# A transformer layer on one core: the beginning written out by hand, the next batch's latents transposed later, and the last weight loads moved

## The chip, the cores and the metric

The kernel runs on one NeuronCore of a Trainium2 chip. The metric is the device time of one execution in microseconds (us); the median of several runs counts, and lower is better.

## The reference

The layer works on 8 batches of 512 tokens with 512 features, in float32: a layer norm, a multi-head attention with low-rank latents, a residual, a second layer norm, a gated feed-forward network (FFN), and a second residual. Cut to what matters:

```python
b, s, _ = hidden_states.shape                    # 8, 512; hidden_states is the normed x
q    = rmsnorm(hidden_states @ wq_a.T, q_norm_w)      # 384 latents for the queries
q    = (q @ wq_b.T).reshape(b, s, 16, 192)            # 16 heads: 128 plain, 64 rotary
kv   = hidden_states @ wkv_a.T                        # 128 latents and 64 rotary
kv_c = rmsnorm(kv[..., :128], kv_norm_w)
k_pe = rope(kv[..., 128:])                            # one rotary key, shared by the heads
kv_x = (kv_c @ wkv_b.T).reshape(b, s, 16, 256)        # per head: 128 key, 128 value
attn = softmax(concat(q_nope, rope(q_pe)) @ concat(k_nope, k_pe).T * SCALE)
x    = x + (attn @ v).reshape(b, s, 2048) @ wo.T
# second half: x + down(silu(gate(norm(x))) * up(norm(x))), weights rounded to fp8 e4m3
```

## The kernel before

**Weights are folded.** The up-projections of keys and queries are multiplied together once per head (`fold_q`, tile `wa`), so that a head's queries are formed directly from the 384 latents and scored against the 128 key latents. In the same way the value up-projection and the output projection are multiplied (`fold_o`, tile `wst`). A group `g` is four heads; its `wst` is stored to DRAM in batch 0 and loaded again by every later batch (`load_wst`, four pieces, two buffers).

**The attention is one long list of steps.** A step is one tile of 128 queries of one head of one batch: `at(b, h, t)` is its number, 8 x 16 x 4 = 512 steps. Each step issues a score tile (`scores`: three matmuls on TensorE into a PSUM tile `sc`, a row maximum on VectorE, an exponential on ScalarE), and, at the start of the next step, `rest`: reciprocal, scaling, and a block-wise transpose on VectorE into `block`. After every second step `send` writes `block` to a DRAM scratch (`way<-block`) and reads it back in four pieces (`prT<-way`), which finishes the transposition of the probabilities. All of these transfers are issued by SP, in order, and each `prT` issue waits until its `way` has landed. Six steps after a head's last tile `attend` multiplies the values with `prT` (`av`).

**Other work is attached to steps by hand.** `put(i, f)` appends a piece of work to step `i`, and under a manual schedule the engines get their instructions in exactly that order. Once per batch the *next* batch's latents are formed this way: `center`, `transpose_x` and `project_x` (tile `lr_ps`) at heads 7, 8, 11 and 12; `norms` at head 13; `scale(t)` on VectorE at (13, 2) for the first two token tiles and two steps later for the other two; and one step after `scale` its `transpose_l(t)`: four TensorE transposes into a PSUM tile `lat_pt`, which ScalarE copies into `lat`. All single-bank PSUM tiles (`sc`, `av`, `qn_ps`, `qpe_ps`, `lr_ps`, `lat_pt` and others) share one pool of six buffers. The output products of a group (`z_ps`, `u_ps`, `v_ps`) have two further buffers.

**The beginning** (latents of batch 0, first folds, first rotary part) stands ahead of the manual schedule, so the framework's scheduler orders it. Its loads all go through SP: the first token tile of `x`, the four chunks of the latent weights `wlr`, then the other three tiles of `x`, then the rest. There is one standard deviation for all four tiles, and `xT` has one buffer.

**The end.** While the last batch's last heads run, SP also loads the last group's `wst` pieces and the first FFN weights (`load_ffn`: four tiles `wg`, one behind each group, then `wu`). Two gate tiles of the FFN (`pg<-yh,wg`) are issued on TensorE ahead of the last head's `attend`.

The lines that place this work are:

```python
put(at(b - 1, 13, 2) + t // 2 * 2, p["scale"], t)            # VectorE
put(at(b - 1, 13, 3) + t // 2 * 2, p["transpose_l"], t)      # TensorE, ScalarE
put(at(b, G * g + 3, 3) - 6 + 2 * k, f)                      # piece k of wst
put(at(B - 1, G * g + 3, 1), self.load_ffn, "wg", g, wp, f"wa{g}")
```

Of the kernel before, what the change touches and what calls it, by code (L numbers as in the profile page):

```python
# [43 lines left out]
P = 128  # L44
# [42 lines left out]
class Layer:  # L87
# [45 lines left out]
    def ln_stats(self, x, small):  # L133


        nc = self.nc
        st = small.tile([P, NT, 6], F32, tag="ln_st", name="ln_st")
        mv = small.tile([P, NT, 2], F32, tag="ln_mv", name="ln_mv")
        sd = small.tile([P, NT], F32, tag="ln_sd", name="ln_sd")
        rstd = small.tile([P, NT], F32, tag="ln_rstd", name="ln_rstd")  # L140

        def moments(t):
            nc.vector.bn_stats(st[:, t, :], x[:, t, :])
            nc.vector.bn_aggr(mv[:, t, :], st[:, t, :])

        def deviation():
            nc.scalar.activation(sd, mv[:, :, 1], AF.Sqrt, bias=self.eps_ln)

        def deviation_inverse():
            nc.vector.reciprocal(rstd, sd)  # L150

        return moments, deviation, deviation_inverse, mv, rstd

# [116 lines left out]
    def attention(self):  # L270
        tc, nc, ins, wp, xp = self.tc, self.nc, self.ins, self.wp, self.xp
        with ExitStack() as ctx:
# [21 lines left out]

            x = xp.tile([P, NT, H], F32, tag="x", name="x")
            wlr = self.wlr
            nc.sync.dma_start(x[:, 0, :], hidden(0)[:, 0, :])
            for c in range(NC):
                nc.sync.dma_start(wlr[:, c, :], ins["wlr"][:, c, :])
            for t in range(1, NT):  # L300
                nc.sync.dma_start(x[:, t, :], hidden(0)[:, t, :])
            xs, toks = {0: x}, {0: wp.tile([P, NT, RQ + 2 * DR], F32, tag="tok", name="tok")}
            qnw, knw, knr = self.load_w("qnw"), self.load_w("knw"), self.load_w("knr")
            self.gs, self.us = self.load_w("gs"), self.load_w("us")
# [114 lines left out]
            def latents(b):  # L419


                lat = xp.tile([P, NR + 1, S], F32, tag="lat", name=f"lat_{b}", bufs=2)
                kvt = hp.tile([P, NT, RKV], F32, tag="kvt", name=f"kvt_{b}")
                kpe = hp.tile([P, 2, S], F32R, tag="kpe", name=f"kpe_{b}")


                tok = toks.pop(b)
                x = tok if b else xs[0]
                ss = sp.tile([P, 2, NT], F32, tag="ss", name="ss", bufs=1)
                rms = sp.tile([P, 2, NT], F32, tag="rms", name="rms", bufs=1)  # L430
                got = {}
                moments, deviation, deviation_inverse, mv, rstd = self.ln_stats(x, sp)

                def center(t):
                    got[t] = hp.tile([P, H], F32, tag="xn", name="xc", bufs=1)
                    nc.vector.tensor_scalar(got[t], x[:, t, :], mv[:, t, 0:1], None, ALU.subtract)

                def transpose_x(t):
                    pt = self.ln_transposed(got.pop(t), ps_r)
                    got["xT"] = hp.tile([P, NC, P], F32, tag="xT", name="xT", bufs=1)  # L440
                    nc.scalar.copy(got["xT"], pt)

                def project_x(t):
                    xT = got["xT"]
                    for k, (lo, hi, n) in enumerate(((0, RQ, RQ), (RQ, RL, RKV))):
                        ps = ps_r.tile([P, hi - lo], F32, tag="r", name="lr_ps")
                        for c in range(NC):
                            nc.tensor.matmul(  # L448
                                ps, xT[:, c, :], wlr[:, c, lo:hi], start=c == 0, stop=c == NC - 1
                            )  # L450

                        r = rstd[:, t : t + 1]
                        if k == 0:
                            nc.vector.tensor_scalar(tok[:, t, :RQ], ps, r, None, ALU.mult)
                        else:
                            nc.vector.tensor_scalar(kvt[:, t, :], ps[:, :RKV], r, None, ALU.mult)
                            for d in (RQ, RQ + DR):
                                nc.vector.tensor_scalar(tok[:, t, d : d + DR], ps[:, RKV:], r, None, ALU.mult)
                        nc.scalar.activation(
                            ps[:, :n], ps[:, :n], AF.Square, scale=r, accum_out=ss[:, k, t : t + 1]  # L460
                        )

                def norms():
                    for k, n in enumerate((RQ, RKV)):
                        nc.scalar.activation(
                            rms[:, k, :], ss[:, k, :], AF.Sqrt, bias=self.eps_rms, scale=1.0 / n
                        )

                def norms_inverse():
                    nc.vector.reciprocal(rms, rms)  # L470

                def scale(t):
                    nc.vector.tensor_scalar(
                        tok[:, t, :RQ], tok[:, t, :RQ], rms[:, 0, t : t + 1], None, ALU.mult
                    )
                    nc.vector.tensor_scalar(
                        kvt[:, t, :], kvt[:, t, :], rms[:, 1, t : t + 1], None, ALU.mult
                    )

                def transpose_l(t):  # L480
                    pt = ps_r.tile([P, NR + 1, P], F32, tag="r", name="lat_pt")
                    for r in range(NR):
                        nc.tensor.transpose(pt[:, r, :], tok[:, t, r * P : (r + 1) * P], self.ident)
                    nc.tensor.transpose(pt[:, NR, :], kvt[:, t, :], self.ident)
                    nc.scalar.copy(lat[:, :, t * P : (t + 1) * P], pt)

                def rotary():
                    pt = ps_r.tile([P, NT, P], F32, tag="r", name="kpe_pt")
                    for t in range(NT):
                        nc.tensor.transpose(pt[:, t, :], tok[:, t, RQ:], self.ident)  # L490
                    r = rope(pt.rearrange("p t s -> p (t s)"), SCALE)
                    nc.scalar.copy(kpe[:, 0, :], r)
                    nc.gpsimd.tensor_tensor(kpe[:, 1, :], r, kpe[:, 0, :], ALU.subtract)

                pieces = {
                    f.__name__: f
                    for f in (
                        moments, deviation, deviation_inverse, center, transpose_x, project_x,
                        norms, norms_inverse, scale, transpose_l, rotary,
                    )  # L500
                }
                return pieces, (lat, kvt, kpe)
# [152 lines left out]
            def put_q(b, h):  # L655

                i = at(b, h)
                if h % 2 == 0:
# [3 lines left out]
                            put(i - 5 + k, f)  # L662

                    put(i - 6, rotary_part)
                put(i - 4, project, b, h)


            p0, state["latents", 0] = latents(0)
            p0["moments"](0), p0["center"](0)
            for t in range(1, NT):  # L670
                p0["moments"](t)
            p0["deviation"](), p0["deviation_inverse"]()
            for t in range(NT):
                p0["transpose_x"](t)
                if t + 1 < NT:
                    p0["center"](t + 1)
                p0["project_x"](t)
            p0["norms"](), p0["norms_inverse"](), p0["scale"](0)
            for t in range(NT):
                p0["transpose_l"](t)  # L680
                if t + 1 < NT:
                    p0["scale"](t + 1)
            load_q(0)
            times = load_pe(0)
            cs_s = self.load_w("cs")
            fold_q(0)
            times()
            load_q(1)
            p0["rotary"]()
            for f in project_pe(0, 0):  # L690
                f()
            project(0, 0)
            fold_q(1)
            load_q(2), load_q(3), load_o(0)


            for b, h in ((b, h) for b in range(B) for h in range(NH)):
# [35 lines left out]
            for b in range(1, B):  # L733
                for g in range(NG):
                    for k, f in enumerate(load_wst(b, g)):
                        put(at(b, G * g + 3, 3) - 6 + 2 * k, f)
                for k, f in enumerate(load_x(xs, b, hidden(b), xp, "x")):
                    put(at(b, 5) + k, f)

# [15 lines left out]
            def put_latents(b):  # L755
# [7 lines left out]
                put(at(b - 1, 13, 1), p["norms_inverse"])  # L763
                for t in range(NT):
                    put(at(b - 1, 13, 2) + t // 2 * 2, p["scale"], t)
                    put(at(b - 1, 13, 3) + t // 2 * 2, p["transpose_l"], t)
                put(at(b - 1, 14, 2), p["rotary"])

            def put_ffn():
# [10 lines left out]
                    put(at(b - 1, 0, 1) + 2 * k, f)  # L780
                put(at(b - 1, 3), *((put_latents, b) if b < B else (put_ffn,)))
            for g in range(NG):
                put(at(B - 1, G * g + 3, 1), self.load_ffn, "wg", g, wp, f"wa{g}")
            put(at(B - 1, NH - 1, 3) + 4, self.load_ffn, "wu", 0, wp, "wst", 2)

            self.gates = {}
# [3 lines left out]
            )  # L790

            with tc.manual_schedule():
                prT = block = rest = None
                for i in range(len(steps) + 19):
                    if rest:
# [144 lines left out]
```

## Time and profile before

| what | us |
|---|---|
| median of 3 runs | 2797.75 |
| the 3 runs | 2793.24, 2797.82, 2797.75 |
| the profiled execution, its own time | 2792.89 |
| its span, first to last instruction | 2791.1 |
| TensorE (PE) busy | 2725.8 (98%) |
| VectorE (DVE) busy | 1883.9 (67%) |
| ScalarE (ACT) busy | 898.1 (32%) |
| GpSimd (POOL) busy | 597.8 (21%) |

The span is 1.8 us shorter than the execution's own time. The attention fills the span up to about 2270 us, the FFN the rest. A float32 matmul is two records of the trace, so "x6" behind a matmul group means three matmuls. PE's busy time is an upper bound, because ends of pipelined matmuls are modelled; the list of waits shows where PE stood still.

### The profile page before, as it was taken

Reading aid. Unit: us, or ns where it says so; the run is one execution under the profiler, and the core shown is the slowest. Engines: PE = TensorE matmul, PEld = TensorE weight load, DVE = VectorE, ACT = ScalarE, POOL = GpSimd, SP = SyncE. Lnnn points to the kernel's source line nnn. Section 1 sums busy time; section 2 is a strip of 40 time slices with the busy share of each in tenths; the row PEclk is TensorE's granted clock in tenths of the full one; section 3 lists DMA queues with packets and bytes.
Section 4 is the critical chain, followed back from the end, with each engine's and each line's share of the span. In section 5 each row is a group of like instructions: output and inputs, shape, how many; then the busy total and the mean of one; then the engine's idle time right before and its main releaser. Section 6 shows DMA issues by size and latency. Waiting matters only on the chain.

```text
span 2791.1 us, 29188 instructions
## 1 busy us (share of the span) xinstructions
PE 2725.8 (98%) x9264; PEld 1720.1 (62%) x9264; DVE 1883.9 (67%) x3680; ACT 898.1 (32%) x1956; POOL 597.8 (21%) x629
## 2 busy tenths in 40 slices
PE   8999999999999999999999999999999989999999
PEld 4565555555556555555555555555555568888887
DVE  5766787778777877787778777877777723433332
ACT  3333333333333323333333333333332323332332
POOL 1221222212221222122212221222111122222222
PEclk9999999999999999999999999999999999999999
DMA  3654465456544654465456545654565542111110
GB/s 115 210 193 157 160 205 169 153 162 202 166 157 162 205 161 157 161 207 162 153 166 204 165 145 172 206 166 144 175 199 174 186 172 82 61 65 61 65 64 19
DMA packets 262377, 426.07 MB, mean 153 GB/s; under 512 B 29648, under 2 KB 192592, under 8 KB 260688
## 3 DMA queue, kind: packets, MB, share of 16 engines
q1 hardware_dynamic: 262224, 424.21, 47.1%
q8 instruction: 74, 1.21, 0.2%
q14 instruction: 79, 0.65, 0.1%
HBM read 248.99 MB, written 175.11 MB: 152 GB/s over the span
## 4 chain that ended last, share of the span: by engine, by line
PE 86%; DVE 8%; ACT 2%; DMA 2%; issue 1%; SPq 0%; POOL 0%; ACTq 0%; DVEq 0%; POOLq 0%
PE av L578 13%; PE sc L555 13%; PE qn_ps L543 10%; PE u_ps L623 7%; PE sc L557 7%; PE pu L261 6%; PE pd L865 6%; PE pg L261 6%; PE qpe_ps L511 6%; PE lr_ps L448 4%; PE v_ps L623 3%; PE z_ps L623 2%; DMA way<-block 2%; DVE pr L567 2%; DVE nmax L559 1%; DVE block L167 1%
## 5 line engine op out<-in xcount | busy, mean ns | idle before, releaser
L562 ACT ACTIVATE pr<-sc,nmax 128x512 f32<-128x512 f32 x512 | 351.8, 687 | 1278.3 <-DVE nmax L559 1274.5
L557 PE MATMUL sc<-kpe,qpe 128*128 128x512 f32 x1024 | 526.3, 595 | 2.1 <-DVE qpe L531 2.1
L555 PE MATMUL sc<-lat,qn 128*128 128x512 f32 x1024 | 523.1, 592 | 0.0
L578 PE MATMUL av<-prT,kvt 128*128 128x512 f32 x1024 | 462.5, 594 | 13.1 <-DMA prT<-way 10.5
L559 DVE TENSOR_REDUCE nmax<-sc 128x1 f32<-128x512 f32 x512 | 338.6, 661 | 120.3 <-PE sc L557 120.1
L167 DVE STREAM_TRANSPOSE block<-pr 128x512 f32<-128x512 f32 x512 | 364.3, 712 | 26.7 <-DMA way<-block 9.2
L543 PE MATMUL qn_ps<-lat,wa 128*128 128x512 f32 x768 | 352.0, 594 | 0.0
L567 DVE TENSOR_SCALAR pr<-pr,rden 128x512 f32<-128x512 f32 x512 | 338.6, 661 | 18.0
L557 PEld LDWEIGHTS sc<-kpe,qpe 128*128 128x128 f32 x1024 | 194.4, 190 | 247.4 <-issue 243.5
L578 PEld LDWEIGHTS av<-prT,kvt 128*128 128x128 f32 x1024 | 194.5, 190 | 210.1 <-issue 196.3
L414 POOL TENSOR_TENSOR roped<-rope_own,rope_sw 128x512 f32<-128x512 f32 x72 | 91.2, 1267 | 961.6 <-DVE rden L566 860.4
L555 PEld LDWEIGHTS sc<-lat,qn 128*128 128x128 f32 x1024 | 189.2, 190 | 136.3 <-issue 112.2
L543 PEld LDWEIGHTS qn_ps<-lat,wa 128*128 128x128 f32 x768 | 145.8, 190 | 135.8 <-issue 124.1
L853 POOL TENSOR_TENSOR fl<-fuse,fh 128x512 fp32r<-128x512 f32 x96 | 125.9, 1312 | 383.1 <-ACT fh L852 383.1
L849 DVE SCALAR_TENSOR_TENSOR fuse<-pu,us,gate 128x512 f32<-128x512 f32 x96 | 71.9, 749 | 193.0 <-PE pu L261 190.0
L566 DVE RECIPROCAL rden<-den 128x1 f32<-128x1 f32 x512 | 81.4, 159 | 159.6 <-ACT pr L562 152.2
L76 POOL TENSOR_TENSOR q_r<-raw,q_m 128x256 f32<-128x256 f32 x72 | 66.2, 919 | 556.7 <-DVE q_m L74 361.5
L511 PE MATMUL qpe_ps<-lat,wqp 128*128 128x512 f32 x384 | 175.2, 592 | 0.0
L261 PE MATMUL pu<-yh,wu 128*128 128x512 f32 x384 | 150.0, 391 | 0.0
L261 PE MATMUL pg<-yh,wg 128*128 128x512 f32 x384 | 149.6, 390 | 0.0
L261 PE MATMUL pu<-yl,wu 128*128 128x512 f32 x384 | 149.4, 389 | 0.0
L261 PE MATMUL pg<-yl,wg 128*128 128x512 f32 x384 | 149.4, 389 | 0.0
(115 smaller groups left out, 3697.1 us busy)
## 6 DMA issues: line engine op xcount, KB each, us to landing
way<-block SPq DMA_DIRECT2D x256, 512.0 KB, 2.8
prT<-way SPq DMA_DIRECT2D x1024, 128.0 KB, 2.8
wst<-wst_d SPq DMA_DIRECT2D x56, 512.0 KB, 4.4
wst<-wst_d SPq DMA_DIRECT2D x56, 384.0 KB, 3.9
x<-in_hid SPq DMA_DIRECT2D x60, 256.0 KB, 3.5
x<-x SPq DMA_DIRECT2D x16, 512.0 KB, 4.4
out<-o SPq DMA_DIRECT2D x32, 256.0 KB, 2.0
wst_d<-wst SPq DMA_DIRECT2D x8, 896.0 KB, 4.6
```

The source lines that it names most:

```text
L167: self.nc.vector.transpose(out[:, :, :, i : i + Q].rearrange("p c k i -> p k c i"), x.rearrange("p (k c j) -> p k c j", c=NQ, j=Q),)
L261: self.nc.tensor.matmul(ps, self.ffn_w[name, i][:, c * P : (c + 1) * P], y[k][:, c, :], start=c == 0 and k == 0, stop=c == NC - 1 and k == 1,)
L511: nc.tensor.matmul(ps, wqp_s[g][:, r, pj * P : (pj + 1) * P], lat[:, r, :], start=r == 0, stop=r == NR - 1)
L543: nc.tensor.matmul(ps, wa_s[g][:, j, r, :], lat[:, r, :], start=r == 0, stop=r == NR - 1)
L555: nc.tensor.matmul(sc, qn[:, q], lat[:, NR, :], start=True, stop=False)
L557: nc.tensor.matmul(sc, qpe[:, h % 2, q], kpe[:, part, :], start=False, stop=part == 1)
L559: nc.vector.tensor_reduce(nmax, sc, AX.X, ALU.max, negate=True)
L562: nc.scalar.activation(pr, sc, AF.Exp, bias=nmax, accum_out=den)
L567: nc.vector.tensor_scalar(pr, pr, rden, None, ALU.mult)
L578: nc.tensor.matmul(av, kvt[:, kt, :], prT[:, :, :, kt, :], start=kt == 0, stop=kt == NT - 1)
L623: nc.tensor.matmul(got[name][:, t, :], ops[p][left][:, t * P : (t + 1) * P], w[:, p, right, :], start=first and t == 0 and p == 0, stop=la ...
L865: nc.tensor.matmul(pd, f[:, i, t * P : (t + 1) * P], w["wd", i], start=i == 0 and f is fh, stop=i == NI - 1 and f is fl,)
```

## The change

- **Transposes.** `transpose_l` of the first two tiles goes from step (13, 3) to (14, 0), behind that step's other work; that of the last two stays at step (14, 1).
- **The beginning.** It becomes a function `first()` under the manual schedule. The `x` tiles are loaded by SP and the `wlr` chunks by ScalarE's queue, alternately. Sixteen transposes of the identity matrix are put on TensorE first. The statistics are formed tile by tile (`normed`); the projection of a tile is split into its two parts, with the next tile's transposes between them, and `xT` gets two buffers. `scale` of all tiles, `fold_q(0)` and `rotary` precede the four `transpose_l`; the queries of head 1 are projected before the first step.
- **Late loads.** The last group's `wst` pieces are issued 8 steps earlier in the last batch, and the last `wg` tile after the last head's transfers instead of in its middle.

```diff
-        def deviation():
-            nc.scalar.activation(sd, mv[:, :, 1], AF.Sqrt, bias=self.eps_ln)
+        def deviation(t=slice(0, NT)):
+            nc.scalar.activation(sd[:, t], mv[:, t, 1], AF.Sqrt, bias=self.eps_ln)
...
-            nc.sync.dma_start(x[:, 0, :], hidden(0)[:, 0, :])
-            for c in range(NC):
-                nc.sync.dma_start(wlr[:, c, :], ins["wlr"][:, c, :])
-            for t in range(1, NT):
+            for t in range(NT):
                 nc.sync.dma_start(x[:, t, :], hidden(0)[:, t, :])
+                nc.scalar.dma_start(wlr[:, t, :], ins["wlr"][:, t, :])
...
-                    got["xT"] = hp.tile([P, NC, P], F32, tag="xT", name="xT", bufs=1)
+                    got["xT", t] = hp.tile([P, NC, P], F32, tag="xT", name="xT")
...
-                put(i - 4, project, b, h)
-            p0, state["latents", 0] = latents(0)
...
-            project(0, 0)
-            fold_q(1)
-            load_q(2), load_q(3), load_o(0)
+                if b or h > 1:
+                    put(i - 4, project, b, h)
+            def first():
+                p, state["latents", 0] = latents(0)
+                for _ in range(4):
+                    pt = ps_r.tile([P, NC, P], F32, tag="r", name="warm")
+                    for c in range(NC):
+                        nc.tensor.transpose(pt[:, c, :], self.ident, self.ident)
+                def normed(t):
+                    p["moments"](t), p["deviation"](slice(t, t + 1)), p["deviation_inverse"](slice(t, t + 1))
+                    p["center"](t)
+                normed(0)
+                p["transpose_x"](0)
+                normed(1)
+                for t in range(NT):
+                    p["project_x"](t, (0,))
+                    if t + 1 < NT:
+                        p["transpose_x"](t + 1)
+                    if t + 2 < NT:
+                        normed(t + 2)
+                    p["project_x"](t, (1,))
+                p["norms"](), p["norms_inverse"]()
+                for t in range(NT):
+                    p["scale"](t)
+                fold_q(0)
+                p["rotary"]()
+                for t in range(NT):
+                    p["transpose_l"](t)
+                rotate, hi, lo = project_pe(0, 0)
+                rotate()
+                fold_q(1)
+                project(0, 0)
+                hi()
+                project(0, 1)
+                lo()
+            load_q(0), load_q(1)
             times = load_pe(0)
             cs_s = self.load_w("cs")
             times()
+            load_o(0)
...
-                        put(at(b, G * g + 3, 3) - 6 + 2 * k, f)
+                        late = (b, g) == (B - 1, NG - 1)
+                        put(at(b, G * g + 3, 3) - (14 if late else 6) + 2 * k, f)
...
-                    put(at(b - 1, 13, 3) + t // 2 * 2, p["transpose_l"], t)
+                    put(at(b - 1, 14) + t // 2, p["transpose_l"], t)
...
-                put(at(B - 1, G * g + 3, 1), self.load_ffn, "wg", g, wp, f"wa{g}")
+                i = at(B - 1, G * g + 3, 1) if g < NG - 1 else at(B - 1, NH - 1, 3) + 3
+                put(i, self.load_ffn, "wg", g, wp, f"wa{g}")
...
             with tc.manual_schedule():
+                first()
+                load_q(2), load_q(3)
                 prT = block = rest = None
```

More of the change, by code (lines that the diff above doesn't have):

```diff
@@ L144, in moments, with deviation_inverse @@
             nc.vector.bn_aggr(mv[:, t, :], st[:, t, :])
-        def deviation():
-            nc.scalar.activation(sd, mv[:, :, 1], AF.Sqrt, bias=self.eps_ln)
-        def deviation_inverse():
-            nc.vector.reciprocal(rstd, sd)
+        def deviation(t=slice(0, NT)):
+            nc.scalar.activation(sd[:, t], mv[:, t, 1], AF.Sqrt, bias=self.eps_ln)
+        def deviation_inverse(t=slice(0, NT)):
+            nc.vector.reciprocal(rstd[:, t], sd[:, t])
         return moments, deviation, deviation_inverse, mv, rstd
@@ L439, in transpose_x, with project_x @@
                     pt = self.ln_transposed(got.pop(t), ps_r)
-                    got["xT"] = hp.tile([P, NC, P], F32, tag="xT", name="xT", bufs=1)
[L441 to L445, printed above, removed]
+                    got["xT", t] = hp.tile([P, NC, P], F32, tag="xT", name="xT")
+                    nc.scalar.copy(got["xT", t], pt)
+                def project_x(t, parts=(0, 1)):
+                    xT = got["xT", t]
+                    for k in parts:
+                        lo, hi, n = ((0, RQ, RQ), (RQ, RL, RKV))[k]
                         ps = ps_r.tile([P, hi - lo], F32, tag="r", name="lr_ps")
@@ L664, in put_q @@
                     put(i - 6, rotary_part)
-                put(i - 4, project, b, h)
-            p0, state["latents", 0] = latents(0)
[L669 to L683, printed above, removed]
+                if b or h > 1:
[33 more added lines that the diff above has]
+                lo()
@@ L684, in attention @@
+            load_q(0), load_q(1)
             times = load_pe(0)
             cs_s = self.load_w("cs")
-            fold_q(0)
             times()
[L688 to L691, printed above, removed]
-            project(0, 0)
-            fold_q(1)
-            load_q(2), load_q(3), load_o(0)
+            load_o(0)
             for b, h in ((b, h) for b in range(B) for h in range(NH)):
```

## The prediction

> **What bounds the kernel now.** I read the page first, then TensorE's own waits, then the timeline around the longest of them, and last the first 50 us. The page's first and second parts:
>
> ```profile
> PE 2725.8 (98%) x9264; PEld 1720.1 (62%) x9264; DVE 1883.9 (67%) x3680; ACT 898.1 (32%) x1956; POOL 597.8 (21%) x629
> PE   8999999999999999999999999999999989999999
> ```
>
> PE is the bound nearly everywhere. No matmul is taken away, so only places where PE stands still, or runs slowly, can give time. The waits of PE alone are short reading:
>
> ```profile
> PE lat_pt L483 <- DVE x L473: 28.1, 8, 4.3
> PE av L578 <- DMA prT<-way: 10.5, 2, 10.1
> PE u_ps L623 <- DVE x L627: 5.9, 8, 0.8
> PE ln_pt L159 <- DVE xc L436: 5.0, 1, 5.0
> PE lr_ps L448 <- ACT xT L441: 3.7, 4, 1.6
> ```
>
> The columns are total us, times, and the longest. The first is the latents' transposes waiting for `scale`, in each of the 7 batches that prepare another; the second is almost all one wait, in the last head. Per batch, PE's timeline in batch 1 shows:
>
> ```profile
> 555.38 1.03 PE L557 MATMUL sc<-kpe,qpe 128*128 128x512 f32 x2
> 560.75 0.87 PE L483 MATMUL lat_pt<-ident,x 128*128 128x128 f32 x3 [4.34 <-DVE x L473]
> 561.41 0.42 PE L484 MATMUL lat_pt<-ident,kvt 128*128 128x128 f32 x1
> ...
> 562.48 2.65 PE L623 MATMUL z_ps<-wst,o 128*128 128x256 f32 x8
> 564.96 1.89 PE L623 MATMUL u_ps<-wst,o 128*128 128x256 f32 x8
> ```
>
> PE is idle for 4.34 us and then slow: these two tiles of transposes take 560.75 to 562.48 = 1.73 us, the same eight at 575.34 only 0.87; `z_ps` takes 2.48 to the next start, `u_ps`, the same size, 1.73. The last head:
>
> ```profile
> 2228.01 8.33 DMA way<-block
> ...
> 2238.72 5.98 DMA way<-block
> 2249.52 5.70 PE av L578 x8
> ```
>
> These are pieces of the chain that ended last (start, length). The `way` of the last head's first half takes 8.33 us to land, where the page's median is 2.8; SP's timeline has a `wst` load at 2227.01 and the 768 KB `wg` at 2227.48 right in front of it. SP cannot issue the second half, ready at 2232.2, before 2238.72.
>
> [...] half speed right after the 4.34 us, and a granted clock of 0.50 in 2245 to 2250. [...] The trace: one issue takes 0.42 to 0.43 us on SP.
>
> **Part A, the transposes.** In the changed program `z_ps`, `u_ps`, a score tile and `qn_ps` stand ahead of the first pair of `lat_pt`. With before's durations from 556.4, when PE ran dry: `z_ps` starts at once, but its second matmul needs head 11's output, which ScalarE copies until 557.5 (its copy starts at 556.88, behind two table loads of 1.28): 0.7 idle. Then `z_ps` to 558.9, `u_ps` 560.6, `sc` 561.9, `qn_ps` 564.5. `scale` of these tiles ends at 561.3 and nothing on DVE ahead of it waits for PE: no wait left. The PSUM buffers they take were released by 556.9 and 557.5. The second pair, unmoved in PE's order, follows at 570.1 instead of 575.34; its `scale`, which before stood behind two waits of DVE for `z_ps` and `u_ps` (1.93 and 1.04), ends about 567.4. The next batch's `qpe_ps` at 572.3 needs ScalarE's copies of this pair, ready about 572.1: a margin of only 0.2, and the place to watch. So the saving is 575.34 - 570.1 = 5.2 us: 4.34 idle + 0.86 slow transposes + 0.75 slow `z_ps` - 0.7. Five other batches have the same 4.3: 6 x 5.2 = 31.4. The first has only 2.1 of waits, and no slow stretch: 2.1. **A = -33.5**, between -20 (half of the idle time comes back as another wait) and -39 (no 0.7).
>
> **Part B, the late loads.** The four `wst` pieces go behind four earlier sends. There they wait for PE's last use of the old buffer, an `u_ps` at 2172.64; SP comes to them after 2184, so nothing queued behind them on SP is held, and each adds its 0.43 of issue beside a queue that has gaps. `wg` goes behind the last `prT`. Then: `block` of half one at 2226.35, `way` lands 2.8 later, four `prT` issues take 1.75: 2230.9. Half two: `block` at 2232.2, landed 2235.0, issues to 2236.7, last landing about 3 later: 2239.7. PE finishes its gate tiles at 2239.4, so the 10.1 wait becomes 0.3 and PE stays warm: `av` takes 3.43 instead of 5.53. What is late next: `z_ps` needs the copy of `av` by ScalarE (0.59), and the two `pu` that hid this before now come after; 0.85 more idle. `wu` is now behind `wg` too: 2.3 MB after 2239.7 at the 308 GB/s that `wu` alone reached (1.57 MB from 2249.4 to 2254.5) land at 2247.4; the first `pu` comes at about 2251. The moved `wg` itself is used only for gates 9 to 11. **B = -9.8 - 2.1 + 0.9 = -11**, between -4 and -13.
>
> **Part C, the beginning.** Added: 16 transposes (first ones: 1.09 for four, so 4.4 us, from 1.4 to 5.8), while PE has nothing to do. New on the path: the table load (1.28) and a square root now stand between the first statistics and the first `xc`. `x` landed at 3.36; with a `wlr` chunk beside it I take 4.0. Then statistics 0.9, table 1.28, root 0.3, reciprocal 0.2, centring 0.5, transposes 0.6 to 1.1, copy 0.58: the projections start at about 8.5, against 6.72. Each tile takes 4.15 on PE plus 0.45 of transposes with no wait between (before: 5.32 a tile): 8.5 + 4 x 4.15 + 3 x 0.45 = 26.5, and 28.2 if PE starts cold; before 29.77. I take 27.3: 2.5 gained. After it ScalarE's order matters. `rotary`'s copy of `kpe` now stands ahead of the four copies of `lat`, so these wait for root and `scale` (4.3), the fold on DVE (0.87), rope (1.9), POOL (1.27) and that copy (0.6), and take 2.2: 11.2 us after the projections; before they were done 5.3 after. PE idles about 6 us and is cold: `qpe_ps` then takes about 4.6 (as `qn_ps` took 4.42 at 45.21), the second fold 0.7, `qn_ps` of both heads 5.2, first scores and third fold 2.1: step 1 begins 23.9 after the projections, at 51.2. Before it began at 50.03. **C = +1.2**, between -3 (all warm) and +4. `wqp` and `cs` move behind one more pair of `wqn`, `wkn` on SP: landed by about 18, needed after 32, nothing.
>
> **Sum.** -33.5 - 11 + 1.2 = -43.3. From the profiled execution's own 2792.89 that is 2749.6. Two of the three runs shown took 5 us more than it and one the same, so I add 2: **2751.5 us**.
>
> **The rivals.** R1, the wait moves: DVE lags PE by up to 7 us here (`sc` of 554.92 gets its maximum at 562.58), so PE, let loose, runs into six full PSUM buffers. For it: DVE is 73% busy in that stretch; against it: buffers traced above are free. Half of A lost: about 2768. R2, the last head's two sends stay serial and slow for another reason, such as the copy of `prT`: B only -4, about 2758. R3, the slower side: the `lat` copies come late at every batch's `qpe_ps`, the 0.2 us margin turned negative on ScalarE's in-order queue. A stall there costs its length[...]. It decides once it exceeds 43.3 / 7 = 6.2 us a batch; at 8 us with 1.6 of cold running 7 x 9.6 = 67, thus 2751.5 + 67 = 2818. Against it: ScalarE is idle for over 1.5 us before most of its work there. R4, the change doesn't do what it says at the start: PE is cold throughout. That is inside C's bounds, 2754.
>
> **How the numbers follow.** Forecast (with R4) 0.78, R1 0.11, R2 0.07, R3 0.04. The range 2740 to 2768 takes in A without its 0.7 and C at its best below, R1 and R2 above; R3 is left out. A measurement of this kernel can tell about 0.2% (5.6 us) from no change. Faster by more: 0.95; within: 0.02; slower: 0.03 (R3 in its worse part).
>
> **What would show it.** In PE's waits of the changed kernel `lat_pt` <- `scale` is gone, and a wait of `z_ps` for ScalarE's copy of 0.6 to 0.7, six times, stands in its place; `z_ps` after it runs at 1.73. `av` <- `prT` is under 1 us and the last `way` lands within 3.5. Step 1's scores start between 47 and 54. I am wrong if a new wait of over 2 us per batch stands at `sc` or `qpe_ps`, or if `pu` waits for `wu`.

## The result, and the profile after

The changed kernel takes **2751.56 us** in the median of four runs (2751.33 to 2753.26); the kernel before, beside it, takes 2797.78 (2793.24 to 2799.86). The ratio is 0.9838, with a 95% interval from 0.9821 to 0.9855. The predicted time was 2751.5. The profiled execution took 2751.33, with a span of 2749.5, which is 41.6 less than the span before.

The page's first and second parts, for TensorE (PE), after:

```profile
PE 2717.8 (99%) x9280; PEld 1714.4 (62%) x9280; DVE 1883.2 (68%) x3683; ACT 896.1 (33%) x1958; POOL 597.8 (22%) x629
PE   8999999999999999999999999999999999999999
```

The weak slice near the end is gone; the weak first slice is still there. PE's waits after (total, times, longest) say the same place by place:

```profile
PE qpe_ps L511 <- ACT lat L485: 6.1, 1, 6.1
PE u_ps L623 <- DVE x L627: 5.9, 8, 0.8
PE z_ps L623 <- ACT o L581: 4.3, 7, 0.7
PE ln_pt L159 <- DVE xc L435: 2.7, 1, 2.7
PE av L578 <- DMA wv<-in_wv: 2.3, 1, 2.3
PE av L578 <- DMA prT<-way: 1.7, 2, 1.2
```

The 28.1 us of `lat_pt` for `scale` and the 10.5 us of `av` for `prT` have left the list or shrunk to 1.7. Two waits are new: the small one of `z_ps`, and one of 6.1 us of `qpe_ps` in the beginning. PE's timeline of batch 1 after shows the small one:

```profile
556.78 0.60 PE L623 MATMUL z_ps<-wst,o 128*128 128x256 f32 x2
558.04 1.56 PE L623 MATMUL z_ps<-wst,o 128*128 128x256 f32 x6 [0.66 <-ACT o L581]
559.44 1.89 PE L623 MATMUL u_ps<-wst,o 128*128 128x256 f32 x8
...
565.06 0.49 PE L483 MATMUL lat_pt<-ident,x 128*128 128x128 f32 x3
...
572.90 2.74 PE L511 MATMUL qpe_ps<-lat,wqp 128*128 128x512 f32 x6
```

PE goes on to `z_ps` instead of standing at `lat_pt`. It pays 0.66 for ScalarE's copy, and everything behind runs at full speed: `u_ps` starts 1.40 after the rest of `z_ps`, and the granted clock is 1.00 from 550 to 565 us, where before it was 0.50 over the first two `lat_pt` and 0.69 over `z_ps`. `qpe_ps`, the next step's reader of the latents, has no bracket, so it does not wait. The last head in the chain that ended last, after:

```profile
2201.26 2.62 DMA way<-block
...
2209.66 3.69 PE av L578 x8
```

The last `way` lands in 2.62 instead of 5.98, and `av` takes 3.69 instead of 5.70 (granted clock 1.00, before 0.64).

How far each place moved against before tells the parts apart. Step 1's scores start at 53.49 instead of 50.14: +3.3 for the beginning. Batch 1's step 55 starts at 555.46 instead of 554.92, so batch 0's own transposes, predicted at 2.1, gave 2.8. Step 58 starts at 571.58 instead of 576.21: from +0.54 to -4.63, which is 5.2 for one batch. The last head's last scores start at 2194.77 instead of 2225.71 (-30.9), the first steady FFN gate at 2229.63 instead of 2271.07 (-41.4). So, in us: **beginning +3.3, transposes -34.2, late loads -10.5**.

### The profile page after: what moved, and what is told of

It is laid out like the page before. It is cut to its first block, busy times and chain, and to the rows that moved or that the text cites. A ratio compares the mean times of both kernels' runs of the same rounds, so it can differ in the third digit from the quotient of the medians.

```text
span 2749.5 us, 29213 instructions
## 1 busy us (share of the span) xinstructions
PE 2717.8 (99%) x9280; PEld 1714.4 (62%) x9280; DVE 1883.2 (68%) x3683; ACT 896.1 (33%) x1958; POOL 597.8 (22%) x629
## 4 chain that ended last, share of the span: by engine, by line
PE 88%; DVE 7%; ACT 3%; DMA 2%; issue 1%; SPq 0%; POOL 0%; ACTq 0%; DVEq 0%
PE av L578 14%; PE sc L555 13%; PE qn_ps L543 10%; PE u_ps L623 7%; PE sc L557 7%; PE pu L261 6%; PE pd L885 6%; PE pg L261 6%; PE qpe_ps L511 6%; PE lr_ps L448 5%; PE v_ps L623 3%; PE z_ps L623 2%; DVE pr L567 1%; DVE block L167 1%; DMA way<-block 1%; DVE nmax L559 1%
```

## The experiments

**One part alone.** The first four add the parts to the kernel before one by one. `e1_transposes_only`:

```diff
-                    put(at(b - 1, 13, 3) + t // 2 * 2, p["transpose_l"], t)
+                    put(at(b - 1, 14) + t // 2, p["transpose_l"], t)
```

> Only the latents' transposes are moved, in the kernel before. Theory (three separate places that add up: transposes about -34, late loads about -10.5, beginning about +3.3 against the span of before): span 2791.1 - 34.2 = about 2757, no wait of lat_pt for scale, a wait of z_ps for ScalarE's copy of 0.7 us six times, and the 10.1 us wait of av for prT still there. Rival (the parts help each other: without the late loads moved, an earlier TensorE only waits longer in the last head): the av wait grows by what the batches save and the span stays above 2765.

Measured: 2758.67 (2757.1 to 2759.87) against 2796.56 of before, ratio 0.9865 (0.9848 to 0.9881); span 2758.1, 33.0 under before's. In its waits `lat_pt` for `scale` is gone, and the other wait stays:

```profile
PE av L578 <- DMA prT<-way: 9.4, 1, 9.4
...
PE z_ps L623 <- ACT o L581: 3.9, 6, 0.7
```

`e2_loads_only` holds the two edits on `wst` and `wg`, and no other.

> Only the late loads are moved, in the kernel before. Theory: the av wait of 10.1 falls to about 1, av runs at full clock, span 2791.1 - 10.5 = about 2780.5, and the seven waits of lat_pt (28 us) are as before. Rival (the last head is bound by the series block, way, prT and not by the loads): span above 2786 with an av wait over 5 us.

Measured: 2784.25 (2780.38 to 2791.68), ratio 0.9955 (0.9942 to 0.9968); span 2779.2, 11.9 under before's. `lat_pt` still waits 28.1.

`e3_beginning_only` is the changed kernel with both of these edits undone.

> Only the beginning is written by hand, in the kernel before. Theory: it costs 3.3 us: step 1's scores start at 53.5 instead of 50.1, span about 2794.5, qpe_ps waits 6.1 us for the copies of lat. Rival (the beginning gains, and what looks like a loss at step 1 is paid back by head 1's early projection and by loads that land earlier): span 2789 or less.

Measured: 2800.08 (2794.76 to 2803.71), ratio 1.0013 (1.0006 to 1.002); span 2797.5, where 2794.5 was expected. The beginning that was to keep TensorE busy costs time. Its step 1 starts at 53.75, 3.6 later than before's. Of the other 2.8 of its span 1.4 come up to step 40 and 0.9 at batch 1's `z_ps`, which took 3.57 there and 2.65 in before (see the last section).

`e4_old_beginning` is the kernel before with the transposes and the late loads.

> Transposes and late loads are moved, the beginning is left as before. Theory: the changed kernel without its loss, span 2749.5 - 3.3 = about 2746 and median about 2748. Rival (the beginning gains): span 2752 or more.

Measured: 2748.43 (2746.79 to 2751.15), ratio 0.9831 (0.9816 to 0.9845); span 2746.2. That is 44.9 under before's, and 33.0 + 11.9 is 44.9 too; but such a sum of spans of single executions is partly luck, because beginnings and ends vary. The starts of the score tiles in the traces take the span apart (us; step 40 is the first of the eleventh head of batch 0):

| kernel | step 1 starts | step 40 starts | from step 40 to the last head's last scores | from there to the end |
|---|---|---|---|---|
| before | 50.14 | 207.79 | 2017.9 | 565.4 |
| `e2_loads_only` | 49.73 | 207.11 | 2017.7 | 554.4 |
| `e1_transposes_only` | 52.60 | 208.77 | 1983.7 | 565.6 |
| `e4_old_beginning` | 51.60 | 208.64 | 1983.7 | 553.9 |
| `e3_beginning_only` | 53.75 | 212.83 | 2019.4 | 565.3 |
| changed | 53.49 | 211.06 | 1983.7 | 554.8 |

The middle column is the transposes' part: 34.2 us less with them moved, the same in three kernels, whatever the beginning and the loads are. The last column is the loads' part: 10.7 to 11.5 less in these. So the two parts do not touch each other. The first four rows differ by 2.9 at step 1 although the beginning is the same program in them, so the beginning's cost is known less well: about 3 us, by the medians too (3.5 for `e3_beginning_only` over before, 3.1 for the changed kernel over `e4_old_beginning`).

**Where the beginning loses.** `e5_lat_first` exchanges two calls in the changed kernel's `first()`:

```diff
                 fold_q(0)
-                p["rotary"]()
                 for t in range(NT):
                     p["transpose_l"](t)
+                p["rotary"]()
```

> The changed kernel with transpose_l called ahead of rotary, so that on ScalarE the four copies of lat stand ahead of the copy of kpe. Theory (ScalarE's order is what the beginning loses by): the 6.1 us wait of qpe_ps for lat shrinks below 1, TensorE keeps its clock, step 1's scores start at about 46.5 instead of 53.5, span 2749.5 - 7 = about 2742.5. Rival (the rotary chain through VectorE and GpSimd sets the first scores whatever ScalarE's order): step 1 starts after 51 and the span stays above 2747.

Measured: **2746.08** (2744.95 to 2746.55) against 2797.08 of before, ratio 0.9815 (0.98 to 0.9829), the best of all versions run. The timelines, first of the changed kernel, then of this one:

```profile
38.45 0.62 ACT L492 CAST kpe<-roped 128x512 fp32r<-128x512 f32 x1 [6.43 <-POOL roped L413]
38.98 2.04 ACT L485 COPY lat<-lat_pt 128x512 f32<-128x512 f32 x4
41.11 4.74 PE L511 MATMUL qpe_ps<-lat,wqp 128*128 128x512 f32 x6 [6.05 <-ACT lat L485]
```

```profile
35.98 3.32 PE L511 MATMUL qpe_ps<-lat,wqp 128*128 128x512 f32 x6
...
39.43 0.62 ACT L492 CAST kpe<-roped 128x512 fp32r<-128x512 f32 x1 [3.55 <-POOL roped L413]
```

In the changed kernel ScalarE, in order, stands 6.43 us at `kpe`'s copy with four ready `lat_pt` behind it, and PE stands for them. Turned round, the wait is gone, `qpe_ps` is less cold (3.32 for 4.74), and step 1 starts at 46.95, 6.5 sooner; 46.5 was expected.

**Whether transposes warm PE.** `e6_warm_matmul` makes the sixteen first transposes plain matmuls of the same tiles (`nc.tensor.matmul` with the identity as both operands). Each of them is two records of the trace, so they also last longer (5.71 us for 3.68): that run changes length as well as kind. `e7_warm_transposes_long` has 28 transposes (`range(7)` instead of `range(4)`), `e10_warm_transposes_no_gap` 36 (`range(9)`).

> The changed kernel with the sixteen first transposes issued as ordinary matmuls of the identity (transpose flag off), nothing else. Theory (the transposes do not count as activity for TensorE's clock, matmuls do): they take about 6.8 us at half clock, the first eight records of lr_ps take 2.8 instead of 5.17, step 1 starts about 2 us earlier, span about 2747.5. Rival (kind does not matter; what lacks is length, or the gap of 2.7 us behind them undoes it): lr_ps is slow here too, or fast both here and with 28 transposes.

> The changed kernel with 28 instead of 16 first transposes, so that they last to about 7.3 us, just ahead of the first real ones at 7.8. Theory (transposes do not count): the first lr_ps records still take about 5.2 and the span stays at 2749 to 2751. Rival (length and the gap matter, not the kind): lr_ps takes 2.8, span about 2747.

> The changed kernel with 36 instead of 16 identity transposes at the start, so that they end at about 8.0, when the first rows are centred, and TensorE has no gap of over 0.7 us before the projections. If transposes raise the clock like matmuls and the idling before the projections is what lost it again in the run with 28 of them (1.25 and 0.68 us), the first lr_ps takes about 2.9 us instead of 4.5 to 5.2, and step 1's scores come at 51.3 to 52 (53.5 in the changed kernel), span about 2748. If transposes hold it less well than matmuls, the first lr_ps stays at 4.5 to 5.2 and step 1's scores at 52 to 53.5.

PE's timelines at the start, in the order changed kernel, 28 transposes, 36 transposes, 16 matmuls:

```profile
1.37 3.68 PE L675 MATMUL warm<-ident 128*128 128x128 f32 x16 [1.37 <-POOL ident masks.py:199]
7.77 1.11 PE L159 MATMUL ln_pt<-ident,xc 128*128 128x128 f32 x4 [2.72 <-DVE xc L435]
9.56 5.17 PE L448 MATMUL lr_ps<-wlr,xT 128*128 128x384 f32 x8 [0.68 <-ACT xT L440]
```

```profile
1.38 5.41 PE L675 MATMUL warm<-ident 128*128 128x128 f32 x28 [1.38 <-POOL ident masks.py:199]
8.03 0.63 PE L159 MATMUL ln_pt<-ident,xc 128*128 128x128 f32 x4 [1.25 <-DVE xc L435]
9.34 4.46 PE L448 MATMUL lr_ps<-wlr,xT 128*128 128x384 f32 x8 [0.68 <-ACT xT L440]
```

```profile
1.37 5.80 PE L675 MATMUL warm<-ident 128*128 128x128 f32 x36 [1.37 <-POOL ident masks.py:199]
8.00 0.63 PE L159 MATMUL ln_pt<-ident,xc 128*128 128x128 f32 x4 [0.83 <-DVE xc L435]
9.31 2.85 PE L448 MATMUL lr_ps<-wlr,xT 128*128 128x384 f32 x8 [0.68 <-ACT xT L440]
```

```profile
1.37 5.71 PE L675 MATMUL warm<-ident 128*128 128x128 f32 x32 [1.37 <-POOL ident masks.py:199]
8.12 0.66 PE L159 MATMUL ln_pt<-ident,xc 128*128 128x128 f32 x4 [1.04 <-DVE xc L435]
9.45 2.85 PE L448 MATMUL lr_ps<-wlr,xT 128*128 128x384 f32 x8 [0.68 <-ACT xT L440]
```

Read the second number of each `lr_ps` line: eight records of one projection take 5.17, 4.46, 2.85 and 2.85 us. In the changed kernel the sixteen transposes start 0.21 us apart, the last ones too. In the trace with 28 they start 0.21 apart at first and 0.11 apart from the 22nd on; with 36 they are 0.11 apart from the 17th on; and the records of the plain matmuls do the same from the 19th on. So PE's pace nearly doubles while it runs transposes, as it does while it runs plain matmuls, and the sixteen ended ahead of that. The granted clock of the trace does not show this step: it is 1.00 over the changed kernel's first 12 us, slow transposes and slow `lr_ps` included. With 28 the following `ln_pt` is fast too (0.63 for 1.11), but PE then is slow in the first half of `lr_ps`: the granted clock is 0.65 from 8 to 12 us, and 1.00 there with 36. What differs from the runs that stayed fast is the idle time ahead of `ln_pt`: 1.25 us, where it was 0.83 with 36 and 1.04 with the matmuls. A greater length is not what was missing: in `e12_best` below 24 transposes last only 4.38, PE idles 0.87, and `lr_ps` takes 2.85. These are one trace each, and 1.25 is no threshold: the last section shows longer waits with a fast `av` behind them.

The run with 28 transposes met neither of its two expectations whole. Its `lr_ps` and its span of 2751.2 lie near those of the theory that transposes do not count, and the starts of the single transposes refute that theory. The run with matmuls did what its theory said at the beginning (step 1 at 51.23, 2.3 sooner), which is no proof of it, since its length changed too.

The medians are 2748.88 with matmuls (ratio 0.9825, 0.9808 to 0.9841), 2751.51 with 28 transposes (0.9833, 0.9818 to 0.9848) and 2749.7 with 36 (0.9828, 0.9814 to 0.9843). A warm start is worth little: with 36 transposes step 1 starts at 50.88, 2.6 sooner than in the changed kernel, but the span, 2748.4, is only 1.1 shorter. Most of it was given back at one early `av`, by PE's timelines (changed kernel, 36 transposes, `e5_lat_first`):

```profile
107.20 3.67 PE L578 MATMUL av<-prT,kvt 128*128 128x512 f32 x8 [2.27 <-DMA wv<-in_wv]
```

```profile
106.11 5.37 PE L578 MATMUL av<-prT,kvt 128*128 128x512 f32 x8 [2.68 <-DMA wv<-in_wv]
```

```profile
100.98 5.37 PE L578 MATMUL av<-prT,kvt 128*128 128x512 f32 x8 [2.61 <-DMA wv<-in_wv]
```

Of 2.6 us gained, 1.1 are left when this `av` starts, and the cold `av` behind the wait (5.37 instead of 3.67) takes these and more. At step 40 the lead is 0.2, and the rest of the 1.1 comes from a shorter wait in the last head. `e5_lat_first` keeps 5.3 of its 6.5.

**Which late load.** `e8_wst_moved_only` is the changed kernel with `wg` in its old place, `e9_wg_moved_only` with the `wst` pieces in theirs; one run each.

> The changed kernel with the last wg load put back to its old place, in the middle of the last head's sends; the wst pieces stay early. Theory (wg is the transfer that holds the way of the last head's first half, 768 KB of the 1.15 MB in front of it): way lands about 5 us late, av waits 5 to 8 us for prT, span 2755 to 2759. Rival (the wst pieces did the harm): av waits under 2.5 and the span stays below 2752.

> The changed kernel with the two up-projection weight loads of the last head back on SP ahead of the last two probability sends (384 and 512 KB), the first gate weights' load still moved behind them: the complement of the run in which only the up-projection loads were moved. If each load ahead of the sends costs by its own bytes, the averages of the last head wait about 4 to 6 us for probabilities, and the span is 2753.5 to 2756 (2749.5 of the changed kernel plus 4 to 6). If it is the last load in the queue alone that delays the sends (so that the gate load, 4 us of it, was most of the part), the span is under 2752.

Measured: spans 2753.5 and 2757.4, or 4.0 and 7.9 over the changed kernel's. The chains of the last head, first with `wg`, then with `wst` in its old place:

```profile
2197.43 6.75 DMA way<-block
...
2206.08 3.46 DMA way<-block
```

```profile
2197.32 4.83 DMA way<-block
...
2204.52 5.95 DMA way<-block
...
2216.29 5.16 PE av L578 x8
```

With `wg` ahead of the sends the first half's `way` takes 6.75; with the `wst` pieces both halves are slow, and `av` waits 7.6 and runs cold (5.16; 3.69 with `wg` in its old place).

These spans do not give each load's price. `e8_wst_moved_only` is already 2.0 us behind the changed kernel at step 40, long before either load, and no more than that at the last scores; from there to the end it takes 556.7, where the changed kernel takes 554.8. Kernels with both loads moved and the same FFN take from 553.7 (`e5_lat_first`) to 557.7 (`e6_warm_matmul`) there, so a price of `wg` is not shown, though its effect on one `way` is. `e9_wg_moved_only` takes 562.8, 8.0 more than the changed kernel and outside of that range: most of the part is due to the `wst` pieces. That is against the theory of `e8`, which gave `wg` most of the harm and expected 2755 to 2759; of `e9`'s expectation the upper end was too small by 1.4. That 4.0 + 7.9 is the 11.9 of `e2_loads_only` is chance.

**Towards a better version.** `e11_best_beginning` has the exchange of `e5_lat_first`, 24 transposes, and

```diff
+                root = self.wp.tile([P, 1], F32, tag="root", name="root")
+                nc.scalar.activation(root, self.eps_ln, AF.Sqrt, bias=self.eps_ln)
                 normed(0)
```

> The changed kernel with its first latents' transposes issued ahead of the rotary embedding, 24 instead of 16 identity transposes at the start, and one square root of a constant on ScalarE ahead of the first rows, so that its table load (1.28 us) runs while the inputs are still on their way. Against the version with only the first of the three (span 2743.1, step 1's scores at 46.95): the table load was on the path from x to the first projection, so 1.3 us go; with the wait of TensorE ahead of the projections shorter by that, the first lr_ps takes 2.9 instead of 5.2 us, of which about 1.7 reach step 1. Span about 2740, step 1's scores at 44 to 45. If the inputs' landing or VectorE's chain of rows sets the pace instead, under 1 us is gained: 2742 to 2743.

Measured: 2747.19 (2745.31 to 2748.25), ratio 0.9819 (0.9804 to 0.9833), no better than `e5_lat_first`. The beginning did a little more than was expected: the table load runs at 2.61, the first `lr_ps` takes 2.85, and step 1 starts at 43.34, 3.6 sooner than in `e5_lat_first`. All of the 3.6 are still there at the attention's end. Then the FFN loses 5.9. Two groups of PE, first of the changed kernel, then of this one (busy time, mean ns of one):

```profile
L261 PE MATMUL pu<-yh,wu 128*128 128x512 f32 x384 | 149.8, 390 | 0.0
L885 PE MATMUL pd<-wd,fh 128*128 128x512 f32 x384 | 149.4, 389 | 0.0
```

```profile
L261 PE MATMUL pu<-yh,wu 128*128 128x512 f32 x384 | 151.0, 393 | 0.0
...
L887 PE MATMUL pd<-wd,fh 128*128 128x512 f32 x384 | 149.4, 389 | 0.0
```

The same gate and up matmuls (`pg`, `pu`), without a wait, are 3 ns longer, in all four groups of line 261: 4.9 of the 5.9 us. The down-projection `pd` is not. The two kernels with the tile `root` have this, the twelve without it do not. In the compiled program `root` takes 32 bytes of each partition, and nearly every tile allocated behind it starts 32 bytes further on, `yh`, `wg` and `wu` among them; `yl` does not move. A slower read from the new places would be a guess, and it is not enough: `wd` and `fh`, which `pd` reads, move by the same 32 bytes, and so do the operands of `av` and `sc`, and none of these matmuls is slower. The cause is open; no run moved a tile by itself.

`e12_best` is `e11_best_beginning` with `z_ps` and `u_ps` of group 2 one step later (`9 if g == 2 else 8` in the list of steps).

> The version before it in this call, with the output matmuls z_ps and u_ps of head group 2 put one step later, behind that step's scores, query projection and the next latents' transposes. The wait of z_ps for ScalarE's copy of o (0.7 us in each of 6 or 7 batches, 4.3 in all) should go. The transposes of the next latents then come about 3.5 us sooner, at about 560.8 in the second batch, where the scaling of their rows was done at 561.3: a wait of about 0.4 us each may come in its place. Span 2 to 4 us under the version before it, about 2736 to 2738. If the transposes' wait eats all of the gain, the two are equal; over it if the later output matmuls hold back the residual sums and so the FFN's start.

Measured: 2749.88 (2749.25 to 2753.69), ratio 0.9833 (0.9816 to 0.9849), 2.7 slower than `e11_best_beginning`. Two of its PE waits:

```profile
PE qpe_ps L511 <- ACT lat L485: 3.0, 6, 0.5
...
PE lat_pt L483 <- DVE x L473: 2.6, 6, 0.4
```

The 0.7 of `z_ps` went, but the transposes came sooner and waited 0.4 for their rows, and `qpe_ps`, without the wait that had given ScalarE time, waited 0.5 for `lat`. It starts ahead of `e11_best_beginning`, and from batch 1 on loses 0.6 a batch against it, 3.5 in all. The listed waits explain about half of that (3.0 and 2.6 more, 4.0 of `z_ps` less). The expected 2736 to 2738 was missed by 10 in the span.

## Why the prediction was right, and where it was not

- **What bounds the kernel.** PE's gaps were the time to be had. The two largest went, one part at a time and together, and the time followed.
- **Part A, -33.5.** Measured -34.2, in the changed kernel and with this part alone. One batch gave the predicted 5.2, the first batch 2.8 instead of 2.1; `z_ps` waits 0.66 (0.7 predicted) and its successors run warm (granted clock 1.00). The margin of 0.2 at `qpe_ps` held; `e12_best` shows how thin it was.
- **Part B, -11.** Measured -10.5, and -11.0 alone. `way` landed in 2.62, and nothing waited for `wu`. The named loads were the cause, but not in the way that the reading of the trace suggests: the `wst` pieces weigh most, and the price of `wg`, the largest transfer in front of the `way`, is not shown.
- **Part C, +1.2.** Measured +3.3 against the one trace of before (step 1 at 50.14, where the prediction has 50.03), about 3 over all runs: the sign was right, the size was not. The term that failed is "I take 27.3" for the end of the projections, a mean between a warm and a cold start: they ended at 30.3, which is 3.8 over its warm sum of 26.5. Two terms make 3.4 of these. The projections started at 9.56 and not 8.5, since `x` landed at 4.55 where 4.0 was taken and the rest of that row of work took 0.5 more than its sum. And PE was cold for nearly the whole first `lr_ps`, 2.3 more than the warm 2.85. After that, 23.2 us passed to step 1, where 23.9 were predicted.
- **Whether transposes warm PE.** The prediction left it open: its 26.5 and 28.2 for the end of the projections stand for a warm and a cold PE. The outcome, a cold `lr_ps` (5.17 for 2.85), looks as if transposes left PE cold, but the runs with 28 and 36 transposes contradict that for these float32 transposes: their starts go from 0.21 to 0.11 us apart. Sixteen were too short, and an idle stretch of 2.7 us followed them.
- **The +2 for the runs.** It was not there: the changed kernel's median is 0.2 over its profiled execution. The parts sum to -43.3 in the prediction and to -41.4 in the trace, so the prediction without its +2 would have been 1.7 too low; two small errors cancelled: that 2751.5 was met to 0.1 is luck. Before's median is 2796.56 over 27 runs (2791.95 to 2801.32): its profiled execution was at the low end. By medians the change is therefore worth 46.2, and the transposes alone 37.9.
- **The rivals.** R1: no new wait stands behind `lat_pt`. R2: the sends became fast. R3: no stall at `qpe_ps` except the one in the beginning. R4 came true in part: PE was cold in the first `lr_ps` (5.17) and again at `qpe_ps` (4.74), and warm between (2.85 in the second and third `lr_ps`); the outcome lies within C's bounds.

## What to carry to other kernels

Let the engine that is the bound do work that is ready while another engine prepares what it needs: a move of a few instructions in order was worth 34 us, with nothing computed differently. Loads that have time must not stand on a queue ahead of transfers that the end waits for: moved away, they gave 10.7 to 11.5 us here. When a beginning is laid out by hand, write down each in-order engine's list and look for an instruction that waits with ready work behind it; here one exchange of two calls gave 5.5 us in the median, more than keeping PE warm did (1.9 with 36 transposes, 2.7 with the matmuls). And where parts are priced by traces of single executions, compare stretches between the same two instructions: here one stretch repeats to 0.1 us, while spans of the same program differ by several.

## What the runs showed of the hardware that was not expected

- **The cold clock is not fixed by the length of a wait.** Waits of 2.61 and 2.68 us ahead of the early `av` (`e5_lat_first` and 36 transposes) were followed by a slow `av` (5.37, granted clock 0.73 from 100 to 104 us and 0.67 from 108 to 112), and waits of 2.27, 2.85 and 2.86 (the changed kernel, `e11_best_beginning` and `e12_best`) by a fast one (3.67, granted clock 1.00). After the same stall at `lat_pt` in batch 1, 4.34 in the kernel before and 4.32 in `e3_beginning_only`, the eight transposes took 1.73 and 1.74, and the same `z_ps` behind them 2.65 and 3.57. What decides it, no run shows. The kernels with that stall spread over 9 to 11 us between runs (8 to 27 runs each), those with the transposes moved over 1 to 5 (4 runs each, so less well known). That the varying cold stretches make this spread fits these numbers, and the mean granted clock of a run goes the same way (before: 0.994 in the fastest run, 2791.95, and 0.991 in the slowest, 2801.32), but it was not tested by itself.
- **A table load cost 1.28 us, with nothing around it.** In `e11_best_beginning` the load starts at 2.61 and the square root at 3.91. In batch 1 of the kernel before, ScalarE's work ahead of the load ends at 554.88, the load starts at 554.90 and the exponential at 556.20: 0.02 on either side of the load.
- **An added tile went with slower matmuls elsewhere.** With one small tile more, and most tiles 32 bytes further on, each of 1536 records of matmuls took 3 ns more, 4.9 us of PE's busy time (603.1 instead of 598.2 over the four groups), while others whose operands moved as far did not. A version of `e11_best_beginning` that keeps the other tiles in place was not run; whether it keeps the beginning's 3.6 us is open.
